# Starting a two-stage convolution: the first plane by halves of channels, batch norm sums ahead of the last row, a smaller memset, and ten additions moved to VectorE

## The chip, the cores and the metric

One core of one Trainium2 chip. The metric is the device time of one execution in microseconds, as the median of several runs. Five engines run their own instruction streams in order: TensorE (PE, with its weight loads, PEld), VectorE (DVE), ScalarE (ACT), GpSimd (POOL) and SyncE (SP, which issues most DMAs).

## What is computed

The input `x` is (8, 256, 56, 56) in float32. Two residual layers follow each other:

```python
# layer 0: group norm (32 groups), then an involution, 7 x 7, 16 groups
ker = einsum('bchw,oc->bohw', gn(x), w_reduce) + b_reduce
ker = einsum('bchw,oc->bohw', ker, w_span) + b_span      # 49 weights per pixel and group
x = x + (ker * patches_7x7(gn(x))).sum(axis=kernel)
# layer 1: group norm, then two 3 x 3 convolutions with ternary weights
v = gn(x)
out1 = relu(batch_norm(conv(v, tq1) + einsum('bchw,oc->bohw', v, tq1[:, :, 1, 1]), g1, b1))
out2 = batch_norm(conv(out1, tq2) + einsum('bchw,oc->bohw', out1, tq2[:, :, 1, 1]), g2, b2)
return x + relu(out1 + out2)
```

`batch_norm` is in training mode: mean and variance are taken over all 8 images and all pixels. So no pixel of `out1` exists before the last row of the first convolution is done, and the same holds for the second. The group norm of layer 1 likewise needs whole images of layer 0's output, though only one image at a time.

## The kernel before

The kernel has three stages one after the other.

**Involution.** The activations lie in SBUF as quarters `xs[b, c]` (image b, 64 of the 256 channels, the 128 partitions holding two halves of the rows). Each quarter is done in ten strips of rows, `ty` = 0 to 9. For a strip, SP loads a patch tile `q` (L728, five buffers), GpSimd adds the constant rim to it (`fill_rim`, L751), and for the last strips ACT copies a further rim (`fill_end`, L764). TensorE then runs the strip's small matmuls (L852) into `pa`; `pick_out` scales the result into `inv` (ACT, L862; a strip with other geometry has further terms on VectorE, L864) and **GpSimd adds `inv` to `xs`** (L868). `gn2_stats` takes the statistics of finished rows on VectorE (L149) and, when the quarter is whole, their sum (L905); `store_x1` writes the quarter to `x1d` in DRAM. The mean of groups goes through two tiny matmuls (L156, L168) into the PSUM tile `pa`, and its variance is formed at L171. A `pin` function fixes the order on the engines within this stage. The last quarter is image 7, channels 192 to 255 (`x_7_3`). GpSimd's other work in this stage includes additions at L800 and, once, `nc.gpsimd.memset(xp, 0.0)` (L1059) for the padded image of the convolutions, 3712 elements per partition.

**Two convolutions.** `conv_phase(i, ...)` is called for i = 1 and 2. Each image is done in two halves, so n runs from 0 to 15. `load` brings the half image into two tiles `raw0`, `raw1`, one for each half `t` of the 256 channels (CT = 2). `transform(n)` normalises them into the padded tile `xp` (the norm function is `norm_x1`, L1049 and L1051, in the first convolution and `norm_y1`, L1067 to L1072, in the second; for n = 0 the channel half t = 0 is normed by ACT and t = 1 by VectorE, two instructions each with the relu), in four classes of rows `f`. Then it combines rows into six planes, made in the order 1, 2, 3, 4, 0, 5, each 128 x 812 with both channel halves side by side: plane 1 is `r = p + q` with `p` and `q` from L387, the others likewise. Each plane is split in two by `keep`:

```python
nc.scalar.copy(hi, r)                                               # L392
nc.vector.tensor_tensor(lo, r, hi.bitcast(F32), ALU.subtract)       # L393
```

TensorE multiplies each plane with weights `wq[k]` in 24 matmuls (L522): two halves of output channels `to`, two parts (hi, lo), two channel halves `t`, three shifts `dx`. So n takes 144 matmuls. VectorE and ACT combine the six results into four rows (L508, L532 to L546). While TensorE works on n, `transform(n + 1)` is made. In this stage a scheduler fixes the order from dependences; nothing is pinned.

**Batch norm.** `statistics` writes sums and sums of squares of each n into the tile `st`, one column per n (L457, on ACT). For the last n, rows 0 to 2 are summed by `last_rows` on ACT into column 15, while VectorE makes the last row of each four from plane 5 (`row_of(3, ...)`, L508). `row_stats` (L471) and `row_sums` (L476 to L482) then put the remaining rows into a seventeenth column, and `batch_norm_params` (L176 to L190, with `rstd_of`, L131 to L145) adds up all 17 columns, forms mean and variance, takes a square root on ACT, a reciprocal with one Newton step on VectorE, and at last scale `sc` and bias `bi`. Every norm of the next stage waits for `bi`.

**Final pass.** Blocks of `y1d`, `y2d` and `x1d` are read back, normed, added and written out (L1098 to L1103).

## Time and profile before

| | |
|---|---|
| median of 3 runs | 2163.53 us (2159.11 to 2166.13) |
| the profiled execution | 2164.76 us, of which the span of its instructions is 2163.0 us |
| involution, start to the first matmul of the first convolution | 0 to 1056.03 us |
| first convolution, from its first matmul to its last | 1056.03 to about 1484.5 us |
| TensorE idle between the two convolutions | 13.58 us |
| second convolution and its batch norm | 1498.08 to about 1933 us |
| final pass | to 2163.0 us |

Times are those of one profiled execution on the device, counted from its first instruction. A group of instructions is shown with its source line, engine, operation, the tiles it writes and reads, the shape, how often it ran, its busy time, the mean duration in ns, and the idle time of its engine just before it with what ended that. "PEclk" is the share of full speed that TensorE's clock was granted. The chain of waits is followed back from the last instruction: at each step to what released it.

### The profile page before, as it was taken

What the parts mean: (1) busy time and instruction counts of PE and PEld (TensorE: products, weight loads), DVE (VectorE), ACT (ScalarE), POOL (GpSimd) and SP (SyncE); (2) the same over time, 40 slices, a digit from 0 to 9 for tenths busy, and PEclk for the clock granted to TensorE, in tenths of its full rate; (3) what the DMA queues carried; (4) which work ended last, traced back from release to release, by engine and by line L of the source; (5) the groups of instructions that cost most, each with busy time, mean ns of one, the idle gap of its engine ahead of it and who ended that gap; (6) DMA issues with size and microseconds to landing.
All of it is one profiled execution on the core that took longest, in us unless ns stands there. A gap on an engine that the chain in (4) does not pass through costs nothing.

```text
span 2163.0 us, 70724 instructions
## 1 busy us (share of the span) xinstructions
PE 1759.3 (81%) x29680; PEld 1632.6 (75%) x29680; DVE 1753.4 (81%) x3337; ACT 1432.2 (66%) x3553; POOL 590.7 (27%) x965
## 2 busy tenths in 40 slices
PE   4988988989899898988699999997999999960000
PEld 4777777878777687777699999997999999960000
DVE  5777978787777868877699999998999999984444
ACT  3877787877767677777366666665566666653344
POOL 0555566555546646666200000000000000000000
PEclk9999999999989999999799999998999999985555
DMA  5667777686767758667733333335323333369999
GB/s 184 212 178 232 220 211 236 195 266 197 244 185 218 239 164 263 191 203 201 254 122 122 122 122 122 122 122 189 118 114 124 124 128 128 124 262 425 429 428 397
DMA packets 156250, 440.06 MB, mean 203 GB/s; under 512 B 63774, under 2 KB 74012, under 8 KB 148508
## 3 DMA queue, kind: packets, MB, share of 16 engines
q1 hardware_dynamic: 150336, 405.50, 55.2%
q10 hardware_dynamic: 5596, 30.03, 3.3%
q8 instruction: 235, 3.85, 0.8%
q14 instruction: 83, 0.68, 0.1%
HBM read 323.28 MB, written 112.20 MB: 201 GB/s over the span
## 4 chain that ended last, share of the span: by engine, by line
PE 68%; DMA 10%; DVE 9%; issue 6%; POOL 3%; ACT 3%; ACTq 0%; SPq 0%; POOLq 0%; DVEq 0%
PE c L522 40%; PE pg L820 14%; PE pa L852 8%; PE pk L713 3%; DMA y1f<-y1d 3%; DMA x1f<-x1d 2%; PE ks L786 2%; DMA out_y<-x1f 2%; POOL q L751 1%; DVE x1f L1102 1%; DVE inv L864 1%; ACT a L824 1%; DMA y2f<-y2d 1%; POOL x L868 1%; DMA q<-in_x_nb 1%
## 5 line engine op out<-in xcount | busy, mean ns | idle before, releaser
L522 PE MATMUL c<-pl,wq 128*128 128x392 f32 x4608 | 857.7, 348 | 14.9 <-ACT pl L392 14.9
L522 PEld LDWEIGHTS c<-pl,wq 128*128 128x128 f32 x4608 | 855.7, 190 | 16.7 <-ACT pl L392 15.3
L824 ACT ACTIVATE a<-pg,bt 126x126 f32<-126x126 f32 (+1 forms) x2048 | 530.1, 469 | 110.1 <-PE pg L820 109.5
L820 PE MATMUL pg<-kr,wl 64*126 64x140 f32 (+1 forms) x6144 | 466.1, 296 | 41.2 <-issue 16.4
L820 PEld LDWEIGHTS pg<-kr,wl 64*126 64x126 f32 x6144 | 405.5, 198 | 67.2 <-issue 24.3
L852 PE MATMUL pa<-a,q 126*32 126x48 f32 x17024 | 290.4, 215 | 67.0 <-issue 52.6
L852 PEld LDWEIGHTS pa<-a,q 126*32 126x32 f32 x17024 | 242.1, 116 | 135.4 <-issue 83.6
L828 DVE TENSOR_TENSOR a<-pg,bt 126x504 f32<-126x504 f32 (+4 forms) x640 | 280.9, 480 | 54.4 <-PE pg L820 52.8
L868 POOL TENSOR_TENSOR x<-x,inv 128x168 f32<-128x168 f32 x320 | 167.0, 522 | 404.1 <-DVE inv L864 370.7
L864 DVE SCALAR_TENSOR_TENSOR inv<-pa,gn1s,inv 128x168 f32<-128x168 f32 (+1 forms) x384 | 134.2, 351 | 154.6 <-ACT inv L862 151.1
L392 ACT CAST pl<-r 128x812 fp32r<-128x812 f32 x192 | 162.5, 868 | 143.4 <-DVE r L387 122.8
L372 POOL MEMSET xp<- 128x116 f32 x32 | 6.3, 196 | 826.1 <-DVE a L387 826.1
L751 POOL TENSOR_TENSOR q<-q,sides 126x256 f32<-126x256 f32 (+1 forms) x320 | 225.5, 705 | 3.1 <-DMA q<-in_x_nb 3.1
L393 DVE TENSOR_TENSOR pl<-r,pl 128x812 fp32r<-128x812 f32 x192 | 186.6, 998 | 27.6 <-ACT pl L392 26.3
L457 ACT ACTIVATE dummy<-y,nc 128x1568 f32<-128x1568 f32 (+1 forms) x128 | 200.2, 1564 | 4.8 <-DVE y L542 3.5
L862 ACT ACTIVATE inv<-pa,gn1s 128x168 f32<-128x168 f32 x320 | 134.9, 423 | 69.5 <-PE pa L852 49.3
L149 DVE BATCH_NORM_STATS2 st<-x 128x6 f32<-128x392 f32 x256 | 137.8, 554 | 16.4 <-DMA x<-in_x 10.1
L800 POOL TENSOR_TENSOR x<-x,add 128x504 f32<-128x504 f32 (+1 forms) x128 | 127.2, 1024 | 25.4 <-ACT add L794 25.4
L1049 ACT ACTIVATE xp<-raw,gn 128x392 f32<-128x392 f32 (+1 forms) x124 | 82.5, 721 | 61.3 <-DVE a L387 61.0
L1069 ACT ACTIVATE xp<-raw,bi_bn,sc_bn 128x392 f32<-128x392 f32 (+1 forms) x124 | 82.3, 720 | 58.8 <-DVE a L387 57.1
L1100 DVE SCALAR_TENSOR_TENSOR y1f<-y2f,sc_bn,y1f 128x3136 f32<-128x3136 f32 (+2 forms) x20 | 56.6, 2831 | 64.6 <-DMA y2f<-y2d 50.6
L713 PE MATMUL pk<-x,wrn 64*128 64x168 f32 (+1 forms) x1152 | 101.0, 316 | 0.0
(174 smaller groups left out, 1789.2 us busy)
## 6 DMA issues: line engine op xcount, KB each, us to landing
q<-in_x_nb SPq DMA_DIRECT2D x320, 448.0 KB, 4.2
raw<-x1d SPq DMA_DIRECT2D x32, 812.0 KB, 5.9
raw<-y1d SPq DMA_DIRECT2D x32, 812.0 KB, 6.1
x<-in_x SPq DMA_DIRECT2D x64, 392.0 KB, 5.3
x1d<-x SPq DMA_DIRECT2D x64, 392.0 KB, 5.2
y1d<-y SPq DMA_DIRECT2D x30, 784.0 KB, 3.7
y2d<-y SPq DMA_DIRECT2D x30, 784.0 KB, 3.4
y1f<-y1d SPq DMA_DIRECT2D x14, 1568.0 KB, 14.4
```

The lines of the kernel that those rows point to most:

```text
L392: nc.scalar.copy(hi, r)
L393: nc.vector.tensor_tensor(lo, r, hi.bitcast(F32), ALU.subtract)
L457: nc.scalar.activation(dst, v, f, bias=shift[:, to:to + 1], accum_out=stats[:, to, j, n:n + 1])
L522: nc.tensor.matmul(ps[:, to, :NM], wq[k][:, t, dx, to * P:(to + 1) * P], part[:, t, :, dx:dx + W], start=(c == 0), stop=(c == last))
L713: nc.tensor.matmul(ps[h][:, :m * W], wrn[rows, c, :], src[rows, r0:r0 + (m - 1) * PY + 1:PY, :], start=(c == 0), stop=(c == NCQ - 1))
L751: nc.gpsimd.tensor_tensor(v, v, z, ALU.add)
L820: nc.tensor.matmul(dst, wl[rows, c, gp, o:o + NQ], kr[py][rows, px, :], start=True, stop=True)
L824: nc.scalar.activation(dst[:, g + 1, p0 + j], ps[1][:NQ, j * nt + t0:j * nt + t1], AF.Identity, bias=bt[:, c, g + 1, p0 + j:p0 + j + 1])
L828: nc.vector.tensor_tensor(dst[:, g, p0:p0 + n].rearrange("q p t -> q t p"), ps[0][:NQ, t0 * n:t1 * n].rearrange("q (t p) -> q t p", p=n), ...
L852: nc.tensor.matmul(ps[o:o + m, k * w:(k + 1) * w], q[:NQ, k, o:o + m], av[:, t + k, g * w:(g + 1) * w], start=True, stop=True)
L864: nc.vector.scalar_tensor_tensor(iv, parts[:, :, g], scale[:, g:g + 1], iv, ALU.mult, ALU.add)
L868: nc.gpsimd.tensor_tensor(xv, xv, iv.rearrange("p t (y x) -> p y t x", x=PX), ALU.add)
```

## The change

It has four parts.

1. **The first plane by halves of channels.** In `transform(0)` of each convolution, plane 1 is made for t = 0 and then for t = 1: four norms, `p`, `q`, `r`, hi and lo, each on half of the elements. The engine of each norm is set by hand: row class 0 on VectorE and classes 2 and 1 on ACT; class 3 on VectorE for t = 0 and on ACT for t = 1. The 24 matmuls of this plane are put in the order of `t` first, so that 12 of them need only t = 0.
2. **Batch norm summed ahead of the last row.** The columns of `st` are reduced, divided and given the epsilon in `batch_norm_before`, ahead of the last `row_of`; the statistics of the last rows are added to the result, `total`, by a single instruction in `row_sums`. The chain in `batch_norm_params` is shorter, and the subtraction of `shift` stands after the square root.
3. **Zeros of side columns only.** The memset of `xp` covers the first and last column of its rows: 128 elements per partition in place of 3712.
4. **The last additions by VectorE.** The ten additions of `inv` to `xs` in the last quarter run on VectorE; those of all the other quarters stay on GpSimd.

```diff
--- before.py
+++ after.py
@@ -120,7 +120,7 @@
         for name, src in (("g1", g1), ("b1", b1), ("g2", g2), ("b2", b2)))
-    st1, st2 = (const_tile([P, CT, 2, 2 * B + 1], name) for name in ("st1", "st2"))
+    st1, st2 = (const_tile([P, CT, 2, 2 * B], name) for name in ("st1", "st2"))
     nc1, nc2 = (const_tile([P, CT], name) for name in ("nc1", "nc2"))
     mv2 = const_tile([P, B, NCQ, 2], "mv2")
@@ -173,18 +173,28 @@
         nc.vector.tensor_copy(dst[:, :, 0], rs)
         nc.vector.scalar_tensor_tensor(dst[:, :, 1], gm[:, :, 0], -1.0, rs, ALU.mult, ALU.mult)
-    def batch_norm_params(stats, shift, gamma, beta, name):
-        mv = small.tile([P, CT, 2], F32, tag="bn_mv", name=f"bmv_{name}")
-        nc.vector.tensor_reduce(mv, stats, AX.X, ALU.add)
-        nc.vector.tensor_scalar(mv, mv, 1.0 / (B * HW), None, ALU.mult)
-        d = small.tile([P, CT], F32, tag="bn_d", name=f"bd_{name}")
-        nc.vector.tensor_tensor(d, mv[:, :, 0], mv[:, :, 0], ALU.mult)
-        nc.vector.tensor_tensor(mv[:, :, 1], mv[:, :, 1], d, ALU.subtract)
+    def batch_norm_before(stats, pre):
+        nc.vector.tensor_reduce(pre, stats[:, :, :, :2 * B], AX.X, ALU.add)
+        nc.vector.tensor_scalar(pre, pre, 1.0 / (B * HW), None, ALU.mult)
+        nc.vector.tensor_scalar(pre[:, :, 1], pre[:, :, 1], BN_EPS * SCALE * SCALE, None, ALU.add)
+    def batch_norm_params(mv, shift, gamma, beta, name):
+        def vec(tag):
+            return small.tile([P, CT], F32, tag=f"bn_{tag}", name=f"{tag}_{name}")
+        ve, sq, r0, e = (vec(tag) for tag in ("ve", "sq", "r0", "e"))
+        nc.vector.tensor_tensor(e, mv[:, :, 0], mv[:, :, 0], ALU.mult)
+        nc.vector.tensor_tensor(ve, mv[:, :, 1], e, ALU.subtract)
+        nc.scalar.activation(sq, ve, AF.Sqrt)
         nc.vector.tensor_tensor(mv[:, :, 0], mv[:, :, 0], shift, ALU.subtract)
-        rs = rstd_of(mv[:, :, 1], BN_EPS * SCALE * SCALE, name)
+        nc.vector.reciprocal(r0, sq)
+        nc.vector.tensor_tensor(e, r0, r0, ALU.mult)
+        nc.vector.scalar_tensor_tensor(e, e, -0.5, ve, ALU.mult, ALU.mult)
+        nc.vector.scalar_tensor_tensor(e, e, 1.5, r0, ALU.add, ALU.mult)
         sc = const_tile([P, CT], f"sc_{name}")
-        nc.vector.tensor_tensor(sc, rs, gamma, ALU.mult)
+        nc.vector.tensor_tensor(sc, e, gamma, ALU.mult)
         bi = const_tile([P, CT], f"bi_{name}")
         nc.vector.tensor_tensor(bi, mv[:, :, 0], sc, ALU.mult)
         nc.vector.tensor_tensor(bi, beta, bi, ALU.subtract)
@@ -370,17 +380,21 @@
             b, h = n // 2, n % 2
             edge = xp[:, 0, :, 0, :] if h == 0 else xp[:, 1, :, HT, :]
             nc.gpsimd.memset(edge, 0.0)
-            for f in (2, 0, 1, 3):
+            def normed(f, t, engine):
                 r0 = (f - 1) % 4 if h == 0 else f
                 m_ = len(range(r0, RAW, 4))
                 i0 = (r0 + 1 - h) // 4
-                for t in range(CT):
-                    norm(xp[:, f, t, i0:i0 + m_, 1:1 + W],
-                         raws[t].rearrange("p (h w) -> p h w", w=W)[:, r0::4, :], b, t,
-                         nc.vector if n == 0 and t else nc.scalar)
-            def d(k):
-                return xp[:, k % 4, :, k // 4:k // 4 + HT, :].rearrange("p t r w -> p t (r w)")
+                norm(xp[:, f, t, i0:i0 + m_, 1:1 + W],
+                     raws[t].rearrange("p (h w) -> p h w", w=W)[:, r0::4, :], b, t, engine)
+            def d(k, t=slice(None)):
+                return xp[:, k % 4, t, k // 4:k // 4 + HT, :].rearrange("p t r w -> p t (r w)")
+            if n > 0:
+                for f in (2, 0, 1, 3):
+                    for t in range(CT):
+                        normed(f, t, nc.scalar)
             def lin(dst, x, c, y):
@@ -400,12 +414,28 @@
                 return temp(f"r{k}{i}_{n}", "tr", 4)
             p, q = tmp("p"), tmp("q")
-            lin(p, d(2), -4.0, d(4))
-            lin(q, d(1), -4.0, d(3))
-            yield
-            r = res(1)
-            nc.vector.tensor_tensor(r, p, q, ALU.add)
-            keep(1, r)
+            if n == 0:
+                r = res(1)
+                hi, lo = (planes.tile([P, CT, HT * WP], F32R, tag=f"pl{j}",
+                                      name=f"pl{i}_{n}_1_{j}") for j in range(2))
+                for t in range(CT):
+                    for f, engine in ((0, nc.vector), (2, nc.scalar), (3, nc.vector),
+                                      (1, nc.scalar)):
+                        normed(f, t, nc.scalar if t and f == 3 else engine)
+                    t = slice(t, t + 1)
+                    lin(p[:, t], d(2, t), -4.0, d(4, t))
+                    lin(q[:, t], d(1, t), -4.0, d(3, t))
+                    nc.vector.tensor_tensor(r[:, t], p[:, t], q[:, t], ALU.add)
+                    nc.scalar.copy(hi[:, t], r[:, t])
+                    nc.vector.tensor_tensor(lo[:, t], r[:, t], hi[:, t].bitcast(F32), ALU.subtract)
+                out[1] = [v.rearrange("p t (r w) -> p t r w", w=WP) for v in (hi, lo)]
+            else:
+                lin(p, d(2), -4.0, d(4))
+                lin(q, d(1), -4.0, d(3))
+                yield
+                r = res(1)
+                nc.vector.tensor_tensor(r, p, q, ALU.add)
+                keep(1, r)
             r = res(2)
             nc.vector.tensor_tensor(r, p, q, ALU.subtract)
             keep(2, r)
@@ -470,7 +500,7 @@
                 v = y[:, to].rearrange("p (r k) -> p r k", k=4 * W)[:, :, k * W:(k + 1) * W]
                 nc.vector.bn_stats(st[:, to, j], v)
-        def row_sums(n, st):
+        def row_sums(st):
             mv = st[:, :, 2, :2]
             for to in range(CT):
@@ -479,10 +509,12 @@
             nc.vector.tensor_tensor(mv[:, :, 0], mv[:, :, 0], shift, ALU.add)
             nc.vector.tensor_tensor(sq, mv[:, :, 0], mv[:, :, 0], ALU.mult)
             nc.vector.tensor_tensor(mv[:, :, 1], mv[:, :, 1], sq, ALU.add)
-            nc.vector.tensor_scalar(stats[:, :, :, n], mv, 2.0 * HT * W, None, ALU.mult)
+            nc.vector.scalar_tensor_tensor(total, mv, 2.0 * HT * W / (B * HW), total,
+                                           ALU.mult, ALU.add)
         done = iter(())
         nxt, begun = {}, ({}, None)
+        total = const_tile([P, CT, 2], f"total{i}")
         for _ in transform(0, raws, nxt):
             pass
         raws = load(i, 1, src_d)
@@ -514,15 +546,18 @@
             m = {}
             for k in ORDER:
                 ps = ps_c.tile([P, CT, 512], F32, tag="conv", name=f"c{i}_{n}_{k}")
-                for to in range(CT):
-                    c, last = 0, CT * 3 * 2 - 1
-                    for part in cur[k]:
-                        for t in range(CT):
-                            for dx in range(3):
-                                nc.tensor.matmul(
-                                    ps[:, to, :NM], wq[k][:, t, dx, to * P:(to + 1) * P],
-                                    part[:, t, :, dx:dx + W], start=(c == 0), stop=(c == last))
-                                c += 1
+                steps_ = [(to, part, t) for to in range(CT) for part in cur[k] for t in range(CT)]
+                if n == 0 and k == 1:
+                    steps_ = [(to, part, t) for t in range(CT) for to in range(CT)
+                              for part in cur[k]]
+                count, last = [0] * CT, CT * 3 * 2 - 1
+                for to, part, t in steps_:
+                    for dx in range(3):
+                        c = count[to]
+                        nc.tensor.matmul(
+                            ps[:, to, :NM], wq[k][:, t, dx, to * P:(to + 1) * P],
+                            part[:, t, :, dx:dx + W], start=(c == 0), stop=(c == last))
+                        count[to] += 1
                 if final and follow:
                     begun[0][k] = weights(i + 1, k)
                 m[k] = ps[:, :, :NM].rearrange("p o (r w) -> p o r w", w=W)
@@ -554,10 +589,12 @@
                             :, :, :18].rearrange("p o (n s) -> p o n s", s=6)
                         row_stats(moments, y, 0, 0)
                 elif k == 5:
+                    if final:
+                        batch_norm_before(stats, total)
                     row_of(3, m[5], 6.0, d, ALU.add)
                     if final:
                         row_stats(moments, y, 3, 1)
-                        row_sums(n + 1, moments)
+                        row_sums(moments)
                 next(steps, None)
             for _ in steps:
                 pass
@@ -565,7 +602,7 @@
                 (nc.scalar if final else nc.sync).dma_start(
                     dst_d[b][to][:, h * NH:(h + 1) * NH], y[:, to])
             done = statistics(n, y)
-        return begun
+        return begun, total
@@ -865,7 +902,8 @@
                                                ALU.mult, ALU.add)
             y, m = ty * PY, n // PX
             xv = xs[b, c][:, y * W:(y + m) * W].rearrange("p (y t x) -> p y t x", t=TX, x=PX)
-            nc.gpsimd.tensor_tensor(
+            engine = nc.vector if (b, c) == (B - 1, NCQ - 1) else nc.gpsimd
+            engine.tensor_tensor(
                 xv, xv, iv.rearrange("p t (y x) -> p y t x", x=PX), ALU.add)
         queue = [(b, c, ty) for b in range(B) for c in range(NCQ) for ty in range(TY)]
@@ -1056,12 +1094,12 @@
         begun = {k: weights(1, k) for k in ORDER[:3]}, begun
         xp = pad.tile([P, 4, CT, HT + 1, WP], F32, tag="xp", name="xp")
-        nc.gpsimd.memset(xp, 0.0)
-        begun = conv_phase(1, begun, x1_d, norm_x1, st1, nc1, y1_d, True)
-        sc1, bi1 = batch_norm_params(st1, nc1, g1_sb, b1_sb, "bn1")
+        nc.gpsimd.memset(xp.rearrange("p f t r w -> p (f t r) w")[:, :, ::WP - 1], 0.0)
+        begun, total = conv_phase(1, begun, x1_d, norm_x1, st1, nc1, y1_d, True)
+        sc1, bi1 = batch_norm_params(total, nc1, g1_sb, b1_sb, "bn1")
         def norm_y1(dst, src, b, t, engine):
             bias, scale = bi1[:, t:t + 1], sc1[:, t:t + 1]
@@ -1071,11 +1109,11 @@
                 nc.vector.tensor_scalar(dst, src, scale, bias, ALU.mult, ALU.add)
                 nc.vector.tensor_scalar(dst, dst, 0.0, None, ALU.max)
-        conv_phase(2, begun, y1_d, norm_y1, st2, nc2, y2_d, False)
-    sc2, bi2 = batch_norm_params(st2, nc2, g2_sb, b2_sb, "bn2")
+        _, total = conv_phase(2, begun, y1_d, norm_y1, st2, nc2, y2_d, False)
+    sc2, bi2 = batch_norm_params(total, nc2, g2_sb, b2_sb, "bn2")
     with ExitStack() as ph4:
         fa, fb, fc, fd = (ph4.enter_context(tc.tile_pool(name=name, bufs=1))
```

## The prediction

> **What bounds the kernel now.** I read the page's chain of waits first, then the group of the convolutions' matmuls, then the timeline of each engine around the three places where TensorE stands still near a convolution.
>
> ```profile
> PE 68%; DMA 10%; DVE 9%; issue 6%; POOL 3%; ACT 3%; ACTq 0%; SPq 0%; POOLq 0%; DVEq 0%
> ...
> L522 PE MATMUL c<-pl,wq 128*128 128x392 f32 x4608 | 857.7, 348 | 14.9 <-ACT pl L392 14.9
> ```
>
> Two thirds of the chain is TensorE, and the 4608 convolution matmuls stood idle for only 14.9 us, all of it for the first cast of a convolution (1.3 us at 1056, 13.6 us at 1498). Inside the convolutions nothing is to be won: 27 us of 27 are busy. The change can touch three stretches: A, the end of the involution up to the first matmul at 1056.03; B, the 13.58 us between the convolutions; C, batch norm 2 before the final pass. Stretch A in GpSimd's and TensorE's timelines (start, duration, engine, work, idle time before it):
>
> ```profile
> 1027.16 3.19 POOL L1059 MEMSET xp<- 128x3712 f32 x1
> 1030.31 1.50 POOL L800 TENSOR_TENSOR x<-x,add 128x504 f32<-128x504 f32 x2
> 1031.77 0.30 POOL L868 TENSOR_TENSOR x<-x,inv 128x56 f32<-128x56 f32 x1
> 1032.03 0.72 POOL L751 TENSOR_TENSOR q<-q,sides 126x256 f32<-126x256 f32 x1
> 1032.71 0.54 POOL L868 TENSOR_TENSOR x<-x,inv 128x168 f32<-128x168 f32 x1
> ...
> 1042.32 0.72 POOL L751 TENSOR_TENSOR q<-q,sides 126x256 f32<-126x256 f32 x1 [0.53 <-DMA q<-in_x_nb]
> ```
> ```profile
> 1032.80 4.06 PE L852 MATMUL pa<-a,q 126*32 126x48 f32 x181 [5.13 <-POOL q L751]
> ```
>
> TensorE stands 5.13 us behind a memset, then gets one strip per 1.2 us, since rims and additions alternate on GpSimd. The end of A and stretch B, in the chain of waits (start, duration, what):
>
> ```profile
> 1049.45 0.51 POOL x L868
> ...
> 1050.97 0.17 DVE mv L905
> ...
> 1055.11 0.88 ACT pl L392
> ...
> 1056.03 4.29 PE c L522 x12
> ```
> ```profile
> 1484.55 1.04 DVE y L508 x2
> ...
> 1490.34 0.17 DVE bi_bn L190
> ...
> 1494.30 1.00 DVE q L387
> 1495.31 0.91 DVE u L414
> 1496.22 0.92 DVE r L407
> 1497.16 0.88 ACT pl L392
> ```
>
> B is wholly serial: 5.97 us from the last row to `bi`, 7.56 us from there to the first matmul at 1498.08.
>
> **The change part by part.** Durations are those of the profiled execution (2164.76 us, of which 2163.0 are span); it lies 1.2 us above the median.
>
> *A, memset and additions.* The memset writes 128 elements; its nearest row is L372 (116 elements, 0.19 us), so GpSimd wins 3.0 us at 1027.16. In the built program's order the ten additions stand on VectorE behind their `inv`, and GpSimd does the rims 7_3_2 to 7_3_9 without a break. Counting 1027.16 + 0.2 + 1.5 (L800) + 0.2 + 0.3 + 0.7, the first rim is done at 1030.1 instead of 1032.75, and the next follow at 0.7 us, faster than TensorE's strips (0.85 to 1 us). The last three `q` loads wait on SP for a free buffer, that is for a strip: they were issued at 1034.25, 1035.43 and 1036.7, and now at about 1031.0, 1031.9 and 1032.8. What is queued behind them on SP (the two `raw` loads, 1037.79) moves 4 to 5 us, the weights (1038.74) too. With the same time from issue to landing, all from the last `q` to the last `inv` (ACT, 1047.56) moves to about 1043.5. From there to the sum of statistics (1050.88) it took 3.32 us; without the trip to GpSimd (0.51 and two hand-overs) about 2.9: 1046.4. This sum gains 4.5 us.
>
> *A, halves.* From that sum to the first matmul it took 5.15 us, through full-size p, q, u, r and the cast. Half-size operations are not in the trace; between L302 (144 elements, 0.309 us) and L407 (812, 0.997) 406 elements take 0.58, of which successive ones show about 0.49 (full ones 0.915 apart). The half cast is ready about 2 us after the sum, but the first convolution matmul uses the PSUM bank of the last strip and the group norm's little matmuls, and so waits for the variance (L171). That chain is sum, matmul, mean (+1.03), square, matmul, variance, with halves between: +3.3 us. First matmul at 1049.7, 6.3 us earlier. Bounds of A: 8, if the loads land sooner in emptier queues; 2.5, if loads land when they did.
>
> *The locks.* The row that bears on the moved additions, and GpSimd's row beside it:
>
> ```profile
> L302 DVE TENSOR_TENSOR piece_w<-piece_w x64: 307/309/1249, 92.6 to 1001.3; 128x144 f32<-128x144 f32 x64
> ...
> L751 POOL TENSOR_TENSOR q<-q,sides x320: 450/729/853, 34.5 to 1042.3; 126x256 f32<-126x256 f32 x128, 126x128 f32<-126x128 f32 x32
> ```
>
> A VectorE addition of two SBUF tiles takes 0.309 us as a median beside a busy GpSimd, with a worst case of 1.249 (mean 0.436). The Trainium skill ("SBUF — State Buffer", section "Who interferes with whom") speaks against this part: such an instruction shares a read port with a GpSimd instruction that reads SBUF, whoever is first holds it for its whole length, and the other stands still. By the rule each of the eight additions beside rims can wait 0.73 more, 5.8 us in all, and A's gain would fall to 0.5 if none of it is hidden. By the row it is 0.44 each, 4.4 us for ten, on an engine that was busy 4.3 of 13 us (1034 to 1047) and so hidden. I take the row, since rims now run ahead and finish when the last loads land, before the last additions. Both ends stay in the range.
>
> *B, batch norm.* By the built order, reduce, scale and epsilon now stand ahead of or between the two L508; the reduce (0.23) fits in VectorE's 0.51 us wait before L508, the other two cost 0.17 between. Off the chain come L178 (0.32 with its queue), L179 (0.20), L184 (0.08), L135 (0.17) and one multiplication of the Newton step (0.20): 0.97 - 0.17 = 0.8 us.
>
> *B, halves.* From `bi` it was four norms with relu on VectorE (2.9), p, q, u, r (3.7), cast (0.9). Now it is two norms with relu (1.5), p (0.49), q (0.49), one norm of t = 1 that the scheduler put between (0.43), r (0.49), half a cast (0.45), hand-overs (0.4): 4.3 instead of 7.56, a gain of 3.3. ACT's five norms (5 x 0.645 = 3.2) end before the cast is due. The second half is ready at +7.4. TensorE's first 12 matmuls take it to +8.5 if cold, +6.5 if warm (then 0.9 is lost); I take cold. B: 4.0, bounds 2.5 and 4.5.
>
> *C.* Here the built order leaves the reduction behind the last rows' statistics; only L184 and the Newton step move: 0.3 us before DMA-bound work. Later planes: VectorE pays about 0.3 us per convolution for splitting and keeps 0.5 us of lead at its narrowest point of B, by my count; cost nothing, and up to 1 to 3 us if that is wrong.
>
> The clock:
>
> ```profile
> 1044.00:1048.00 4.00, 3.07 (x87) 0.50 1.01 415
> ...
> 1056.00:1060.00 4.00, 3.98 (x12) 0.50 0.99 376
> ...
> 1498.00:1504.00 6.00, 5.92 (x18) 0.50 0.07 30
> 1504.00:1506.00 2.00, 2.00 (x13) 1.00 0.00 0
> ```
>
> Both convolutions start at half clock (0.35 us per matmul instead of 0.185) for 4 to 6 us, costing 2 to 3 us each. An idle time of 5.13 us already gave 0.50 at 1032, so B's shorter gap of 9.5 us saves none of that: zero.
>
> Sum: 6.3 + 4.0 + 0.3 = 10.6 us; the profiled execution becomes 2154, the median 2153 us.
>
> **The rivals.**
>
> *A's gain stays in the loads (0.17).* DMA was at 0.97 from 1034 to 1047, so an earlier `q` or `raw` may land little earlier, or locks eat the lead. For: 3.17 us of TensorE's idle at 1043 end with the last loads. Against: before 1034 DMA is at 0.57, and the earlier loads go in ahead of the weights. A gives 1 to 2.5; total 5.5 to 7: 2157 to 2158.5.
>
> *VectorE falls behind in the first planes (0.13).* It is busy over 25 of each 27 us, so a lost lead comes back slowly, and an earlier start of TensorE uses it up. 2 to 3 us come back in each convolution, in new idle time of L522 after the first 12 matmuls: total 5 to 7, 2157 to 2159.
>
> *The clock stays at half (0.12), the slower side.* Place: plane 1 of both convolutions. Half-planes that arrive late interrupt TensorE, and the warm-up begins anew. For: 1044 to 1048 shows 0.50 at 77% busy. Price: 0.165 us per cold matmul. To lose the gain of 10.6 us takes 65 more cold matmuls beyond the 30 of now, over both convolutions; with all of 288 cold it is 42 us lost. With 130 more it is 21 - 10.6 = 11 us slower: 2174. Against: while cold, TensorE is slow enough that the second half is in time.
>
> *The sums are not ahead.* For batch norm 2 the order shows this already; if batch norm 1's columns come from ACT later than 1484.07, 0.5 us are lost. It is within the range.
>
> **How the numbers follow.** What a measurement of this kernel can tell from no change is about 0.3%, 6.5 us: faster means below 2157. The forecast (0.58) spans 2147 to 2157 and is faster but for 0.03. The first rival is faster for 0.06 of its 0.17, the second for 0.05 of its 0.13, else the same; the third is slower. Faster 0.66, same 0.22, slower 0.12. The range leaves out the third and the low tail: 2147 to 2163.
>
> **What would show it.** In the profile after: first matmul of the first convolution near 1049.7; no wait of 5 us behind L751; the last three `q` issued by 1033; the additions on VectorE under 0.5 us each; idle time before the second convolution 9.5 us instead of 13.58, with 12 matmuls of 0.35 us and no new idle before the thirteenth; idle time of L522 in all about 11 us. Wrong would be: additions of 0.7 us and more, the last `q` landing at 1042 as before, idle time inside n = 0 or 1, or a granted clock of 0.50 beyond the first 20 matmuls.

## The result, and the profile after

| | before | after |
|---|---|---|
| median, 9 runs each | 2162.17 us (2153.31 to 2166.83) | 2152.53 us (2144.61 to 2168.06) |
| ratio | 1 | 0.9962, 95% interval 0.994 to 0.9984 |
| once more, 59 and 22 runs | 2163.75 us | 2152.18 us, ratio 0.9945, interval 0.9929 to 0.9962 |

The change makes the kernel faster by 0.4 to 0.55%, some 8 to 12 us.

The profiled execution of after is the slowest of its nine: its span is 2166.2 us, more than the 2163.0 of before, so the two profiles compared as wholes show no gain. GpSimd's first constant-term addition of the last quarter (L800 before, L837 after) starts at 1024.76 us before and at 1037.83 us after. The two involutions drift apart and together again by up to 4 us from one of the 32 quarters to the next, almost all of it ahead of anything that the change touches. In the twelve profiles of kernels that are the same up to it, the landmark lay between 1014.8 and 1037.8 us. So everything below is read by stretches, from a landmark to the next: **A** from that addition to the first matmul of the first convolution, **B** from the last row on VectorE (L508 before, L540 after) to the first matmul of the second, and the **end**, from the second convolution's last row to the end of the span.

| stretch, us | before | after (first profile, repeat) |
|---|---|---|
| A | 31.27 | 26.97, 26.22 |
| first convolution | 428.52 | 428.86, 428.48 |
| B | 13.54 | 9.20, 9.20 |
| second convolution | 429.26 | 428.36, 428.16 |
| end | 235.63 | 234.99, 235.13 |
| sum | 1138.2 | 1128.4, 1127.2 |

In the page of after, the group of the convolutions' matmuls (count, busy time and mean, then idle time and releaser):

```profile
L557 PE MATMUL c<-pl,wq 128*128 128x392 f32 x4608 | 857.1, 348 | 9.5 <-ACT pl L429 9.2
```

The idle time fell from 14.9 to 9.5 us, and what is left is one gap, B's. No new gap has appeared inside a convolution. B in the chain of waits of after (start, duration, what):

```profile
1493.65 0.57 DVE y L540
1494.22 0.07 DVE total L179
1494.30 0.47 DVE y L540
1494.76 0.08 DVE total L180
...
1498.65 0.17 DVE bi_bn L200
...
1500.76 0.58 DVE q L401
1501.33 0.42 DVE xp L1109
1501.76 0.49 DVE r L428
...
1502.27 0.54 ACT pl L429
...
1502.86 7.26 PE c L557 x29
```

From the last row to `bi` it is 5.16 us (5.97 before), from there to the matmul 4.04 (7.57). The two small instructions between the rows (L179, L180) cost 0.15 us, and one norm of t = 1 stands in the chain (0.42). The second half did not hold TensorE up: 29 matmuls in a row. A, in GpSimd's and in TensorE's timelines of after:

```profile
1040.22 0.28 POOL L1097 MEMSET xp<- 128x128 f32 x1
...
1042.26 3.57 POOL L788 TENSOR_TENSOR q<-q,sides 126x256 f32<-126x256 f32 x5
...
1053.60 0.72 POOL L788 TENSOR_TENSOR q<-q,sides 126x256 f32<-126x256 f32 x1 [1.44 <-DMA q<-in_x_nb]
```
```profile
1043.04 3.83 PE L889 MATMUL pa<-a,q 126*32 126x48 f32 x181 [2.29 <-POOL q L788]
1047.75 1.30 PE L889 MATMUL pa<-a,q 126*32 126x48 f32 x99 [0.88 <-issue]
1049.45 0.53 PE L889 MATMUL pa<-a,q 126*32 126x48 f32 x28 [0.40 <-POOL q L788]
1052.84 0.85 PE L889 MATMUL pa<-a,q 126*32 126x48 f32 x28 [2.86 <-issue]
1055.74 2.99 PE L889 MATMUL pa<-a,q 126*32 126x48 f32 x84 [2.05 <-issue]
```

The wait behind the rim fell from 5.13 to 2.29 us, as it should. But the first two long gaps marked "issue" are nearly as long as before (0.94 and 3.17 then); the experiments below show what they are. The last one, 2.05, is another thing: it belongs to the last `q`, whose rim came at 1053.60. This load set the end of A. In before, and in the repeat of after, the same places read:

```profile
1043.23 0.86 PE L852 MATMUL pa<-a,q 126*32 126x48 f32 x28 [3.17 <-issue]
1044.46 2.99 PE L852 MATMUL pa<-a,q 126*32 126x48 f32 x84 [0.38 <-issue]
```
```profile
1035.12 0.72 POOL L788 TENSOR_TENSOR q<-q,sides 126x256 f32<-126x256 f32 x1 [0.37 <-DMA q<-in_x_nb]
1036.25 0.53 PE L889 MATMUL pa<-a,q 126*32 126x48 f32 x28 [2.94 <-issue]
1037.27 2.99 PE L889 MATMUL pa<-a,q 126*32 126x48 f32 x84 [0.48 <-issue]
```

| us behind the landmark | before | after | repeat |
|---|---|---|---|
| last `q` issued | 11.93 | 10.03 | 8.51 |
| last `q` landed | 17.41 | 15.61 | 14.86 |
| TensorE starts its last 84 matmuls (last two strips) | 19.71 | 17.91 | 17.16 |
| from their end to the convolution's first matmul | 8.57 | 6.07 | 6.07 |

In all three the last 84 matmuls start 2.3 us behind the landing of the last `q`, and so they do in five more of the fourteen profiles; in the other six they start later. ACT's copy of the further rim (L801, 1054.35 in after) and the scalings of two earlier strips behind it lie between the two; that TensorE waits for these scalings is read from the order on ACT and was not tested.

### The profile page after: what moved, and what is told of

Its sections match the earlier page's. It is cut to its first block, busy times and chain, and to the rows that moved or that the text cites. A ratio compares the mean times of both kernels' runs of the same rounds, so it can differ in the third digit from the quotient of the medians.

```text
span 2166.2 us, 70733 instructions
## 1 busy us (share of the span) xinstructions
PE 1761.7 (81%) x29680; PEld 1635.1 (75%) x29680; DVE 1756.3 (81%) x3350; ACT 1436.3 (66%) x3557; POOL 582.5 (27%) x955
## 4 chain that ended last, share of the span: by engine, by line
PE 64%; DMA 10%; DVE 10%; issue 7%; POOL 4%; ACT 3%; SPq 0%; ACTq 0%; POOLq 0%; DVEq 0%
PE c L557 40%; PE pg L857 12%; PE pa L889 7%; PE pk L750 3%; DMA y1f<-y1d 3%; DMA out_y<-x1f 2%; POOL q L788 2%; DMA y2f<-y2d 2%; ACT a L861 2%; POOL x L906 1%; PE ks L823 1%; DVE inv L901 1%; DMA x1f<-x1d 1%; DVE x1f L1140 1%; DVE a L865 1%
## 5 line engine op out<-in xcount | busy, mean ns | idle before, releaser
L906 POOL TENSOR_TENSOR x<-x,inv 128x168 f32<-128x168 f32 x310 | 161.5, 521 | 413.7 <-DVE inv L901 378.9
L837 POOL TENSOR_TENSOR x<-x,add 128x504 f32<-128x504 f32 (+1 forms) x128 | 127.2, 1024 | 25.4 <-ACT add L831 25.4
```

Source lines behind the costliest of these rows:

```text
L906: engine.tensor_tensor(xv, xv, iv.rearrange("p t (y x) -> p y t x", x=PX), ALU.add)
```

## Experiments

The parts one by one, all on the kernel before.

**Memset alone.** Edit: only the line of the memset.

```diff
-        nc.gpsimd.memset(xp, 0.0)
+        nc.gpsimd.memset(xp.rearrange("p f t r w -> p (f t r) w")[:, :, ::WP - 1], 0.0)
```

> Only part 3 (zeros of side columns) on the kernel before. Read by stretches: A from GpSimd's first constant-term addition of the last quarter (L800, 1024.76 before) to the first matmul of the first convolution, 31.27 us before and 26.97 after; B from the last row on VectorE to the first matmul of the second convolution, 13.53 before and 9.21 after. Theory 1 (TensorE's strips at half clock, 1.2 us each, set the pace, so only the earlier start of the rims counts): A falls by 2 to 2.8 us, the last q is issued 2.8 us earlier, and strips keep 1.2 us. Theory 2 (GpSimd's alternation of rims and additions sets the pace): the memset alone gives the same 2 to 2.8, but the strips stay at 1.25 only because of GpSimd. B unchanged in both. A rival, that the loads land when they did: A falls by less than 1.

A was 29.36 us, 1.9 less than before. Strips took 1.12 us each (168 matmuls in 3.37 us) at a granted clock of 0.58; GpSimd's rims, alternating with additions, came 1.18 to 1.29 us apart, and TensorE waited 0.29 us for one of them. In the changed kernel the rims come 0.7 us apart, and yet the strips took 1.18 us at a clock of 0.64. There TensorE's cold clock sets the pace, not GpSimd: at a clock of 1.00 the next 99 matmuls took 1.30 us, 0.74 us for a strip. The gain of A was a little under what both theories gave.

**Additions alone.**

```diff
-            nc.gpsimd.tensor_tensor(
+            engine = nc.vector if (b, c) == (B - 1, NCQ - 1) else nc.gpsimd
+            engine.tensor_tensor(
```

> Only part 4 (last ten additions by VectorE) on the kernel before. Theory 1 (strips paced by TensorE's half clock): A falls by 0.5 to 1 us, all of it behind the last inv, where the trip to GpSimd goes; the last q is issued when it was. Theory 2 (paced by GpSimd): strips take 0.85 to 1 us, the last three q loads are issued 0.5 to 1 us earlier each after the other, A falls by 1.5 to 2.5. The lock (VectorE and GpSimd keep each other from reading): the additions take 0.7 us and more, A unchanged or longer.

A was 31.79 us: nothing gained, 0.5 lost. The last loads were issued when they were before (9.58, 10.70 and 11.98 us behind the landmark, against 9.49, 10.67 and 11.92). Nine of the ten additions took 0.21 to 0.42 us, one 0.79; only two of the ten ran beside a rim for 0.4 us or more. Behind the last `inv` the trip to GpSimd is gone, but VectorE's order now has norms and a whole `p` ahead of the sum of statistics:

```profile
1048.74 0.99 DVE L387 SCALAR_TENSOR_TENSOR p<-xp 128x812 f32<-128x812 f32 x1
1049.65 0.26 DVE L906 BATCH_NORM_AGGREGATE mv<-st 128x2 f32<-128x24 f32 x1
```

This is VectorE's timeline of that kernel; the sum is at 27.48 us behind the landmark instead of 26.13. Of these 1.35 us the strips, whose last load landed 0.46 us later, account for 0.66. And 0.83 us come back, since `p` and the norms are then done: from the sum to the first matmul it is 4.31 us instead of 5.14.

**Halves alone.** Edit: `transform` and the order of the 24 matmuls, as in the change.

> Only part 1 (first plane by halves of channels, matmuls by t first) on the kernel before. Prediction's step: in A the time from the sum of statistics (L905) to the first matmul falls from 5.15 to 3.3 us, A by 1.8; in B the time from bi to the first matmul falls from 7.56 to 4.1 us. No new idle time of the convolution's matmuls behind the first twelve. Rival (VectorE falls behind in the first planes): 1 to 3 us of new idle inside n = 0 or 1.

From the sum of statistics to the first matmul 3.24 us instead of 5.14, from `bi` to the first matmul 4.03 instead of 7.57, no new idle time. Both to 0.1 us as expected. A as a whole was 28.65, 2.6 less: 1.9 behind the sum, 0.4 between the last strip and the sum, and 0.3 that is scatter of the loads ahead of it.

**Batch norm alone.** Edit: `batch_norm_before`, `row_sums` and `batch_norm_params`, as in the change.

> Only part 2 (batch norm summed ahead of the last row) on the kernel before. Prediction's step: from the last row (L508) to bi 5.2 us instead of 5.97, the rest of B unchanged; from the second convolution's last row to the final pass's first product (L1100) 0.4 us less. A is as before, 31.3 us, and shows how far this stretch repeats by itself; the involution ahead of it may differ by some 10 us.

From the last row to `bi` 5.16 us. A was 31.01 without any edit in it, so this stretch repeats to some 0.3 us. The end was 234.46 us; over all profiles it was 235.6 to 236.4 us in four with the old batch norm (mean 236.0) and 234.5 to 235.6 in ten with the new one (mean 235.0).

Now variants of the changed kernel. **Matmuls in the old order:**

```diff
-                if n == 0 and k == 1:
-                    steps_ = [(to, part, t) for t in range(CT) for to in range(CT)
-                              for part in cur[k]]
```

> The changed kernel, but the 24 matmuls of the first plane in the old order (by output channels first), so that the fourth already needs t = 1. In the changed kernel's trace hi of t = 1 is ready 3.1 us after the first matmul in B and 1.8 us after it in A. If the order is what makes the halves pay: new idle time of 2.1 us behind the third matmul in B and 0.7 us in A, the rest as in the changed kernel. If the cold clock matters more than the order: the same idle time, and on top of it a longer stretch at half clock (1 to 2 us), since the first matmuls come in pieces. If the order is of no account: no idle time over 0.3 us.

The order makes the halves pay: TensorE stood 1.82 us behind the third matmul in B and 0.48 us in A. The first 48 matmuls of the second convolution took 13.08 us; in the profiles of the other kernels, the one with warm-up matmuls below left out, they took 10.3 to 11.6. TensorE's timeline of this kernel:

```profile
1487.01 1.35 PE L554 MATMUL c<-pl,wq 128*128 128x392 f32 x3 [9.23 <-ACT pl L429]
1490.18 40.06 PE L554 MATMUL c<-pl,wq 128*128 128x392 f32 x207 [1.82 <-ACT pl L429]
```

**The constant term by VectorE too,** so that GpSimd's rims start earlier still:

```diff
-                    nc.gpsimd.tensor_tensor(x_, x_, v, ALU.add)
+                    engine = nc.vector if (b, c) == (B - 1, NCQ - 1) else nc.gpsimd
+                    engine.tensor_tensor(x_, x_, v, ALU.add)
```

> The changed kernel, and the four constant-term additions of the last quarter (L837 of the changed kernel, 128 x 504, 1 us each on GpSimd) by VectorE too. TensorE waits 2.29 us behind them for the first rim. Theory 1 (the earlier start of the rims is what pays in A): this wait falls under 0.5 us, the last q loads are issued 2 us earlier, and the first matmul of the convolution comes 1 to 2 us earlier. Theory 2 (the landing of the last loads sets the end of A, and the loads are held up on SP and in flight): under 0.7 us. Theory 3 (VectorE in the way of the strips, or held by GpSimd): additions above 1 us, nothing gained.

The wait behind the rim did fall to 0.25 us, and the first matmul of the convolution came 2.3 us later, not earlier (counted from the last constant-term matmul, which does not depend on the edit: 30.81 us instead of 28.46). None of the theories had named where it went:

```profile
1029.01 0.97 PE L890 MATMUL pa<-a,q 126*32 126x48 f32 x55 [0.25 <-POOL q L788]
1034.91 3.00 PE L890 MATMUL pa<-a,q 126*32 126x48 f32 x126 [4.94 <-issue]
1038.98 2.99 PE L890 MATMUL pa<-a,q 126*32 126x48 f32 x127 [1.07 <-issue]
1045.18 3.61 PE L890 MATMUL pa<-a,q 126*32 126x48 f32 x112 [3.21 <-issue]
```

That is TensorE's timeline: it starts a strip early, and then stands 4.94 us although rims for two further strips lie ready, and 3.21 us once more at the end. In this kernel the first convolution also lost 1.8 us of idle time inside n = 1 and 2. The scheduler had moved a load of `raw` ahead of the last `q` loads, so it is not a clean test of the rims.

**Less traffic behind the last q.**

```diff
-        begun = {k: weights(1, k) for k in ORDER[:3]}, begun
+        begun = {k: weights(1, k) for k in ORDER[:1]}, begun
```

> The changed kernel, but of the first three planes' weights only the first is loaded ahead of the convolution, the other two behind the load of the second half image: 1.5 MB less traffic behind the last q. In the changed kernel the last q took 5.4 us from issue to its rim, and TensorE stands 4.9 us for the last two q. If traffic behind them slows them: 1 us or more less from issue to rim, A shorter by that. If not: A unchanged. The convolution may then wait for the weights of plane 2 (idle time of its matmuls behind the 24th), which is no part of the question.

A was 26.31 us, inside the scatter of the changed kernel (26.2 to 27.3 in four profiles). The 1.5 MB of weights make no difference that stands out of this scatter; 0.31 us of idle time behind the 24th matmul is what it cost.

**Warm matmuls in the gap.**

```diff
+        if i == 2:
+            warm = ps_c.tile([P, CT, 512], F32, tag="conv", name="warm")
+            for _ in range(44):
+                nc.tensor.matmul(warm[:, 0, :NM], wq[1][:, 0, 0, :P],
+                                 wq[1][:, 0].rearrange("p d o -> p (d o)")[:, :NM],
+                                 start=True, stop=True)
         for _ in transform(0, raws, nxt):
```

> The changed kernel, and 44 matmuls of weights with weights, whose result nobody reads, between the two convolutions: TensorE stays busy for 8 of the 9.2 us of B. Theory (B's first 18 matmuls run at half clock because of the gap): granted clock 1.00 from the first matmul of the second convolution, 0.185 us each, 2.3 to 2.8 us less from there to the last row, B itself unchanged. Rival (VectorE is the bound in the first planes): the matmuls are fast, but TensorE then stands behind casts (idle time 1 us behind the twelfth, more behind later planes), and under 1 us is left of it.

The clock was 1.00 from the first matmul, in the windows' rows (stretch, length, PE busy and matmuls, granted clock):

```profile
1487.10:1490.00 2.90, 2.63 (x12) 1.00 0.96 352
1490.30:1494.00 3.70, 3.67 (x18) 1.00 0.09 39
```

The same rows of the changed kernel, at its start of the second convolution:

```profile
1502.80:1506.60 3.80, 3.75 (x11) 0.50 0.86 311
1506.60:1509.00 2.40, 2.40 (x14) 1.00 0.08 35
```

And yet nothing was gained: to the 576th matmul it took 109.16 us, in the two profiles of the changed kernel 108.31 and 108.12. For the first plane the rival holds: TensorE stood 0.54 us behind the twelfth matmul, for the cast of t = 1, and was at the 25th after 5.80 us, where the changed kernel took 6.16 and 5.96. It lost this lead in n = 1 and 2, in the waits of the first two rows here. The other two rows are of the constant-term kernel's first convolution, which starts at a clock of 0.50 (TensorE's waits: what waits, for what, us in all, times, longest):

```profile
PE c L563 <- DVE d L577: 0.6, 1, 0.6
PE c L563 <- DVE y L546: 0.2, 1, 0.2
PE c L557 <- DVE d L571: 0.6, 1, 0.6
PE c L557 <- DVE y L540: 0.2, 1, 0.2
```

These are the same two waits, ahead of the 265th and the 337th matmul both times. In both kernels the scheduler had moved a copy of `e` ahead on ACT, against its place in the changed kernel, and steps of VectorE with it. So the later waits can come from this order and not from the warm clock; that half a clock costs nothing behind the first plane is not shown.

**The additions back on GpSimd.** Edit: the changed kernel with `nc.gpsimd` for all additions.

> The changed kernel with the last ten additions back on GpSimd, so parts 1, 2 and 3 alone. Alone on the kernel before, the additions by VectorE gave nothing (A 31.8 us instead of 31.0 and 31.3). If they give nothing beside the other parts either: A 26.5 to 27.5 us as in the changed kernel (26.3 to 27.3 in four profiles), all times the same. If they pay behind the last inv: there and only there 0.4 to 0.6 us more, A 27 to 28. If GpSimd's alternation counts once the memset is gone: the last loads are issued 1 us later and A is 28 or more. Time 0.3 to 0.6% under the kernel before.

A was 26.20 us, the ratio to before 0.9952 (0.9936 to 0.9969), median 2152.31 us: the changed kernel without its fourth part is as fast as with it.

**The changed kernel again.**

> The changed kernel once more, beside the others of this call. Stretches by the sum of parts (A -4.3, B -4.3, batch norm 2 and final pass -0.5 to -1): 9 to 10 us under the kernel before, a ratio of 0.995 to 0.996, if the involution ahead of them is unchanged. If the involution lost what is gained behind it, as in the first profile of the changed kernel (13 us later at the last constant term): about 1.0.

2152.18 us, ratio 0.9945 (0.9929 to 0.9962), A 26.22. The involution's delay of the first profile was not the change's: here the landmark lies at 1020.1 us.

**One rim earlier.**

```diff
-                surround()
+                surround(PLEAD if m < len(quarters) - 2 else 1)
```

> The changed kernel, and in the last two quarters GpSimd adds each rim one strip earlier (one load instead of two left bare), so that the rim of strip 2 of the last quarter stands ahead of the four constant-term additions. Theory 1 (the start of the rims counts): TensorE's wait of 2.29 us behind the rim is gone or under 1 us, the last loads are issued about 1.2 us earlier, A shorter by about 1 us, B as in the changed kernel. Theory 2 (the flight of the last loads and the code blocks of TensorE set the end of A): under 0.5 us, the wait comes back behind issue or a load. A rim earlier may also wait for its own load: GpSimd idle behind DMA in the last two quarters and up to 3 us lost.

The wait behind the rim was gone, and A was 28.3 us, 1.3 to 2 longer; the ratio to before was 0.9966 (0.9948 to 0.9983). Theory 1 has fallen. The last 84 matmuls start 3.45 us behind the landing of the last `q` here, so something else held them. TensorE's timeline of this kernel:

```profile
1027.91 1.39 PE L889 MATMUL pa<-a,q 126*32 126x48 f32 x111 [1.10 <-DVE inv L901]
1032.24 0.93 PE L889 MATMUL pa<-a,q 126*32 126x48 f32 x57 [2.94 <-issue]
1033.50 1.65 PE L889 MATMUL pa<-a,q 126*32 126x48 f32 x69 [0.33 <-issue]
1037.50 2.93 PE L889 MATMUL pa<-a,q 126*32 126x48 f32 x127 [2.35 <-issue]
1044.26 3.61 PE L889 MATMUL pa<-a,q 126*32 126x48 f32 x112 [3.83 <-issue]
```

The same gaps as in the constant-term kernel. Between the starts of two such gaps TensorE ran exactly 256 instructions, matmuls, weight loads and waits together, in before, after, its repeat and the kernel with the additions on GpSimd. And each gap ends 1.2 to 1.6 us behind the end of a packet of 16 KB on the DMA queue that the page lists as "q8 instruction". The first two gaps of each kernel, in us behind the landmark:

| kernel | 16 KB packet | TensorE goes on |
|---|---|---|
| before | 10.83 to 11.76, 16.14 to 17.10 | 13.04, 18.47 |
| after | 7.50 to 8.65, 12.64 to 13.58 | 9.92, 15.01 |
| constant term by VectorE | 8.20 to 9.08, 12.35 to 13.28 | 10.51, 14.57 |
| one rim earlier | 4.32 to 5.20, 8.40 to 10.50 | 6.61, 11.87 |

This looks like TensorE waiting for its code. **Twice the code** tests it:

```diff
+                        for _ in range(2 if (b, c) == (B - 1, NCQ - 1) else 1):
                             nc.tensor.matmul(ps[o:o + m, ...
```

> The changed kernel with every matmul of the last quarter's ten strips issued twice (the second writes the same result again): 528 matmuls and as many weight loads more, two to three more code blocks of 256 instructions in each 5 us of now. In all profiles TensorE's gaps marked issue in A (0.9 and 2.9 us, 256 instructions apart) end 1.2 to 1.5 us behind a 16 KB packet of the instruction queue. Theory (code blocks arrive too slowly while the DMA engines are full, and set A): the gaps marked issue become four or more, 8 us and more in sum, each ending so behind a packet, and A grows by their sum beyond the matmuls' own 7 to 11 us. Rival (the last loads of q set A, and the gaps only happen to lie there): the gaps do not grow in sum (4 us or less), since the matmuls' own time covers the flight of the loads.

```profile
1026.75 2.80 PE L890 MATMUL pa<-a,q 126*32 126x48 f32 x128 [1.59 <-issue]
1031.62 1.69 PE L890 MATMUL pa<-a,q 126*32 126x48 f32 x127 [2.07 <-issue]
1035.94 2.09 PE L890 MATMUL pa<-a,q 126*32 126x48 f32 x128 [2.63 <-issue]
1040.06 2.89 PE L890 MATMUL pa<-a,q 126*32 126x48 f32 x127 [2.03 <-issue]
1043.88 1.69 PE L890 MATMUL pa<-a,q 126*32 126x48 f32 x127 [0.92 <-issue]
1050.50 2.75 PE L890 MATMUL pa<-a,q 126*32 126x48 f32 x128 [4.92 <-issue]
1054.53 2.83 PE L890 MATMUL pa<-a,q 126*32 126x48 f32 x127 [1.29 <-issue]
1058.45 0.42 PE L890 MATMUL pa<-a,q 126*64 126x32 f32 x5 [1.08 <-issue]
```

Each row of TensorE's timeline but the last is one block of 256 instructions (127 or 128 matmuls, as many weight loads, a wait or two), with a gap ahead of each. The eight gaps make 16.5 us, where the changed kernel had 3.7 in two (4.4 in the repeat), and all eight end 1.3 to 1.6 us behind a packet. A grew from about 26.6 (mean of five profiles of the changed kernel's A) to 42.45, by 16: some 12.8 of it is these gaps, the rest the matmuls' own time less the waits that it covered. The theory of the code blocks holds for this kernel, and the rival has fallen here: longer matmul time did not cover the gaps, and the last `q` landed 7.8 us ahead of the last strips. Here too the scheduler had moved a load of `raw` ahead of the last five `q` loads, which can't add gaps of TensorE 256 instructions apart. For the changed kernel itself it does not follow that code sets A: there the last `q` does, with a code gap ending 2.9 us (first profile) and 1.0 us (repeat) ahead of the last 84 matmuls.

## Why the prediction was right

**The total.** Forecast 2153, measured 2152.53 and 2152.18. The stretches sum to 9.8 to 11 us less than before (1138.2 to 1128.4 and 1127.2), against 10.6 in the sum. That they agree so closely is partly luck: A gave 1.3 to 2 us less than forecast, B 0.3 and the end 0.2 to 0.3 more, and 0.9 to 1.1 us comes from the second convolution, for which nothing was forecast. That one is scatter: with its first plane unchanged it took 428.1 to 429.3 us in four profiles.

**A, memset and rims: right in the start, too large in the end.** The first rim came 2.8 us earlier (forecast 2.7), the wait behind it fell by 2.84. But A's gain was 4.3 to 5.05 us in the two profiles, and not 6.3. The term that was too large is the last `q`: 3.9 us earlier, with the same time to landing, on rims "faster than TensorE's strips (0.85 to 1 us)". It was issued 1.90 us earlier in the first profile and 3.42 in the repeat, it landed 1.80 and 2.55 earlier, and by just that the last 84 matmuls came earlier; what follows them gained 2.50, forecast 2.3. The strips took 1.2 us, and about as much in the profile of before (181 matmuls, or 3.2 strips, in 4.06 us), so buffers came free more slowly than forecast. In the first profile SP also stood 2.15 us in the issue of the second last `q`; in the repeat the last `q` took 6.35 us to land instead of 5.48. The 3.17 us of idle time at 1040, which the prediction took for the flight of the last loads, is a code block. It stands close behind the loads as the next limit: had the last `q` been there, the last 84 matmuls could have started 0.38 us earlier in before, 2.05 in after and 0.48 in the repeat, by the idle time ahead of them.

**A, halves: right.** From the sum of statistics to the first matmul 3.24 us, forecast 3.3; the wait for the variance stands there as described: the cast ended at 1063.82, the variance at 1064.69, the matmul came at 1064.80.

**The moved additions: near in the price, wrong in the worth.** The row came nearer than the rule: in the first profile of after the ten cost 3.7 us, forecast 4.4 by the row. But the reason is another than the one given. Eight additions were to run beside rims; only two did so for 0.4 us or more in the first profile, and three in the repeat. One of the two took 0.64 us, and two of the three 0.72 and 0.77, where all others took 0.22 to 0.42. So where the two engines met, three additions of five were held up, which fits the rule; they seldom met. The worth was put at 0.42 us behind the last strip. There it measured 0.19: 6.07 us from the last strip's end to the first matmul, 6.26 with the additions on GpSimd. A as a whole was 26.20 without them, so nothing of it shows in the time.

**B: right.** 0.8 us for batch norm was measured at 0.81, 3.3 for the halves at 3.5: 4.34 in all, forecast 4.0. The second half came 3.1 us behind the first matmul, as forecast (7.4 less 4.3), and the cold matmuls covered it, as the prediction had assumed; with warm ones TensorE stood 0.54 us there. That B's shorter gap saves nothing of the clock was right too: 0.50 for the first 3.8 us.

**C: too small.** 0.3 us forecast, 1.0 measured between the means of the profiles with old and new batch norm (0.64 and 0.5 from before to the two profiles of after). 0.41 of it lies ahead of the first product of the final pass (5.76 to 5.35 us from the last row); where the rest comes from was not traced.

**The rivals.** Loads that hold A back: half true, the landing of the last `q` took 1.3 to 2 us, up to a third, of A's forecast gain, with code blocks close behind. VectorE behind in the first planes: not in the changed kernel; with warm matmuls TensorE waited for the first plane's second half, and whether the waits of n = 1 and 2 belong to this rival is open. The clock that stays at half: the first twelve matmuls took 3.93 us in the first profile and 3.74 in the repeat, as before (4.09), no more.

## What to carry to other kernels

Where a stage begins with a serial chain and its consumer can start on half of the data, cut the chain in halves and put the consumer's work in the order of the halves: both are needed, since the halves without the order gave 1.8 us back. Before starting a stretch earlier, follow what its last step waits for: here the last load came only 1.8 to 2.6 us earlier, whatever was won in front. In a stretch of small matmuls look also for idle time marked "issue" that comes every 256 instructions: it is no wait for data, and an earlier start does not remove it. And when runs scatter by more than the effect, compare profiles from a landmark behind the scatter.

## What the hardware showed that was not expected

- **TensorE waits for its code, and not only here.** In the profile of before, 48 of the 58 idle times over 0.3 us that are marked "issue" ahead of the first convolution end 1.1 to 1.7 us behind a 16 KB packet of "q8 instruction", and from each to the next it is a whole number of 256 instructions, give or take one. They sum to 63 us (65 in after, 50 of 55), six times what the change gained; how much of that sets the time was not tested. In the last quarter, with the DMA engines 0.86 to 0.97 busy, a block of 256 instructions (16 KB) came every 3.5 to 7 us (with twice the code, where TensorE waited for each), while TensorE used one up in 1.7 to 2.9 us. The Trainium skill ("Runtime: NRT & Kernel Launch", section "Instruction fetch mechanics") describes blocks of that size, whose cost it calls mostly hidden; here TensorE stood 3.7 to 4.4 us for them in the changed kernel's last quarter and 16.5 us with twice the code. That busy DMA engines are the cause was not shown: 1.5 MB less of weights changed nothing beyond scatter.
- **A DMA-issuing instruction of SP can take 2.15 us** instead of 0.33 (the second last `q` of the changed kernel, 2.08 with the memset alone). It ended within 0.1 us of a code gap of TensorE both times; why was left open. In nine of the fourteen profiles one of the last two `q` took 1 us or more to issue.
- **Half clock can cost little.** The second convolution starts with 9 to 17 matmuls at 0.33 us instead of 0.19. With the clock at 1.00 from the start TensorE was only 0.2 to 0.4 us ahead at the 25th matmul, since it then waited for a cast.
